# Where the row maxima of attention logits are read from: PSUM banks in halves, or the SBUF copies in one piece

## The chip, the cores and the metric

The kernel runs on one core of a Trainium2 chip. The metric is device time in microseconds (us). The kernel before has a median of 3184.22 us over three runs (3184.0 to 3186.14). The core's engines run side by side, each through its own queue in order: TensorE (PE, matmuls; its weight loads are shown as PEld), VectorE (DVE), ScalarE (ACT), GpSimd (POOL), and SyncE (SP), which issues the transfers.

## The reference

Input: 8 images of 512 channels and 32x32 pixels, float32. Two pre-activation layers follow each other, each `x + f(groupnorm(x))`:

- Layer 0: a 1x1 convolution with SiLU to 2 x 256 channels, then two bottleneck blocks on 256 channels, and a 1x1 convolution over the four collected results. Each block is a 3x3 convolution with SiLU, an attention over the 1024 pixels with 4 heads of 64 channels, a 1x1 convolution with SiLU, and a residual sum.
- Layer 1: a grouped 1x1 convolution with scaled, masked and permuted weights, brought to one dense 512x512 matrix.

The attention is what matters here. For each head:

```
logits = einsum('bhdi,bhdj->bhij', q, k + r) * HD ** (-0.5)     # 1024 queries x 1024 keys
a = softmax(logits, axis=-1)
out = einsum('bhij,bhdj->bhdi', a, v)
```

The softmax subtracts, for each query, the largest logit over all 1024 keys.

## The kernel before

Everything is float32. An attention is cut into units: `Unit(im, i, hp, half)` handles a pair of heads (hp) and half of the queries (512) of one block of one image. There are 8 x 2 x 2 x 2 = 64 units. The logits of a unit lie transposed, keys on partitions and queries along the columns, in eight key tiles of 128 keys. One key tile is two heads of 512 queries: 1024 columns.

In `logits` (lines 500 to 523) each key tile `t` takes two PSUM banks, one for each head, from the pool `ps_f` of five banks that all matmuls of the kernel share in turn. PE writes both (L511). ACT copies each bank to its half of an SBUF tile `st` (L518; ten `st` buffers in the pool `stp`). From the second key tile on, DVE takes an elementwise maximum into `mx` (L523), one instruction for each head.

After the last key tile, `top` (L531, L532) has PE transpose `mx`, and DVE reduces each transposed piece to the negative maximum over the 128 partitions, `nm`. `spread` (L540) broadcasts that into two PSUM banks of their own, `mb`. For each key tile `soften` (L545) adds `mb` to `st` on DVE, `exponent` (L549) takes the exponential in place on ACT, and POOL adds the result to a running sum `acc` (called `sum` in the profile) in four pieces of 256 columns (L556). `values` (L563) multiplies by v into the accumulator `po`. `finish` (L577, L580) and `divide` (L584, L586) form the denominator and divide.

The main loop works on key tiles in pairs and on two units at once. A step for `t, t+1` issues, in this order: `soften(t)` and `soften(t+1)` of the present unit u, `exponent(t)`, `values` of the pair before, `logits(t)` and `logits(t+1)` of the next unit, and `exponent(t+1)`. So DVE's maxima belong to the next unit while POOL's sums belong to the present one. The ten `st` buffers mean that tiles t and t+1 of the next unit go into the slots of tiles t-2 and t-1 of the present one, which must have been read by `values` and by POOL's sums.

Between the steps, matmuls of other stages are woven in by `advance`, out of a list that `slot_filler` makes for each slot of four units: the convolutions `cv`, `l`, `m2`, the 3x3 convolution of the coming block in a transformed form (`conv3`, L313, products `m`), and its projection. The input transform of `conv3` (`transform`, L280 to L288) is eight DVE instructions of 544 columns that read SBUF only, spread in time by due times of a planner's clock. The order on DVE is partly written down: `in_turn` chains the maxima, the softening and the transform. `act_turn` and `pe_turn` do the same for ACT's copies and exponentials and for PE's attention matmuls. The rest is placed by order of issue.

Dependencies are turned into semaphores automatically. [...] where ACT and DVE both read a bank, the second reader waits for the first, and the bank can be written again when both are done.

Of the kernel before, what the change touches and what calls it, by code (L numbers as in the profile page):

```python
# [17 lines left out]
ALU = mybir.AluOpType  # L18
# [21 lines left out]
def conv_preact_kernel(ctx: ExitStack, tc: tile.TileContext, x, cv1, cv2, mcv1, qkv, mcv2, bn, rw, rh, conv, s_in, t_in, out):  # L40
    nc = tc.nc
# [23 lines left out]
    def pair(p, tag, name):  # L65
        return p.tile([P, 2, HALF], F32, tag=tag, name=name)

    def bank(name):
        return ps_f.tile([P, HALF], F32, tag="bank", name=name)
# [4 lines left out]
    def flat(t):  # L74
        return t.rearrange("p a b -> p (a b)")
# [106 lines left out]
    def in_turn(instruction):  # L182

        if turn:
            tc.add_manual_dep(instruction.ins, turn.pop().ins.name, IN_ORDER, reason="order of VectorE")
        turn.append(instruction)

    def act_turn(instruction):

        if act_last:  # L190
            tc.add_manual_dep(instruction.ins, act_last.pop().ins.name, IN_ORDER, reason="order of ScalarE")
        act_last.append(instruction)
# [3 lines left out]
    def pe_turn(instruction):  # L196

        if pe_last:
            tc.add_manual_dep(instruction.ins, pe_last.pop().ins.name, IN_ORDER, reason="order of TensorE")
        pe_last.append(instruction)  # L200
# [293 lines left out]
    class Unit:  # L494
# [8 lines left out]
        def logits(self, t):  # L503

            if t == 0:
                self.begin()
            lg = [bank(f"lg_{self.name}_{t}_{h}") for h in range(2)]
            for h in range(2):
                r = slice(HD * h, HD * h + HD)
                pe_turn(  # L510
                    nc.tensor.matmul(  # L511
                        lg[h], self.k[r, ts(t, P)], self.q[r, self.hp, ts(self.half, HALF)], start=True, stop=True
                    )
                )
            st = pair(stp, "st", f"st_{self.name}_{t}")
            self.st.append(st)
            for h in range(2):
                act_turn(nc.scalar.copy(st[:, h], lg[h]))  # L518
            if t == 1:
                self.mx = pair(one, "mx", f"mx_{self.name}")  # L520
            for h in range(2 if t else 0):
                so_far = self.st[0] if t == 1 else self.mx
                in_turn(nc.vector.tensor_tensor(self.mx[:, h], so_far[:, h], lg[h], ALU.max))  # L523

        def top(self):

# [621 lines left out]
```

## Time and profile before

| | |
|---|---|
| median of three runs | 3184.22 us |
| the profiled execution | 3188.51 us |
| its span, first to last instruction | 3186.8 us |
| mean granted clock of TensorE | 0.993 |
| PE busy | 3085.9 us (97%) |
| DVE busy | 2050.6 us (64%) |
| ACT busy | 1717.3 us (54%) |
| POOL busy | 1395.3 us (44%) |
| DVE maxima, L523 | 896 instructions of 512 columns |
| POOL sums, L556 | 1792 instructions of 256 columns |

A group line of the profile names the source line, the engine and operation, what is written from what, the shapes and the count; after the first bar stand the busy time in us and the mean of one in ns; after the second bar stands the engine's idle time before these instructions and what ended it. A line of a timeline starts with the start time in us and the duration; several instructions of one kind are merged (x4), and square brackets show idle time of the engine before them, with what ended it. The wait view gives, for an engine and a line, what it waited for: us in total, times, and the longest.

### The profile page before, as it was taken

What the parts mean: (1) busy time and instruction counts of PE and PEld (TensorE: products, weight loads), DVE (VectorE), ACT (ScalarE), POOL (GpSimd) and SP (SyncE); (2) the same over time, 40 slices, a digit from 0 to 9 for tenths busy, and PEclk for the clock granted to TensorE, in tenths of its full rate; (3) what the DMA queues carried; (4) which work ended last, traced back from release to release, by engine and by line L of the source; (5) the groups of instructions that cost most, each with busy time, mean ns of one, the idle gap of its engine ahead of it and who ended that gap; (6) DMA issues with size and microseconds to landing.
All of it is one profiled execution on the core that took longest, in us unless ns stands there. A gap on an engine that the chain in (4) does not pass through costs nothing.

```text
span 3186.8 us, 34171 instructions
## 1 busy us (share of the span) xinstructions
PE 3085.9 (97%) x11668; PEld 1522.9 (48%) x11668; DVE 2050.6 (64%) x2718; ACT 1717.3 (54%) x2347; POOL 1395.3 (44%) x1867
## 2 busy tenths in 40 slices
PE   7999999999999999999999999999999999999999
PEld 3645444454445454454445454454445454453333
DVE  5446576667666676667666676667766676666742
ACT  3255765854655555544656455554656455555631
POOL 2114444446444454445444454355434454455420
PEclk9999999999999999999999999999999999999999
DMA  8851442421233232424233332424233332413366
GB/s 294 287 187 63 154 161 83 149 79 65 88 109 129 93 119 70 148 86 137 89 109 129 119 114 75 139 83 142 90 113 132 110 122 71 145 63 129 110 212 216
DMA packets 142014, 399.35 MB, mean 125 GB/s; under 512 B 13072, under 2 KB 14352, under 8 KB 141840
## 3 DMA queue, kind: packets, MB, share of 16 engines
q1 hardware_dynamic: 141120, 396.94, 36.4%
q8 instruction: 92, 1.51, 0.2%
q14 instruction: 82, 0.67, 0.1%
q10 hardware_dynamic: 720, 0.23, 0.0%
HBM read 317.42 MB, written 79.69 MB: 125 GB/s over the span
## 4 chain that ended last, share of the span: by engine, by line
PE 70%; DVE 7%; ACT 5%; issue 3%; DMA 2%; POOL 1%; ACTq 0%; DVEq 0%; SPq 0%; POOLq 0%
PE m L313 14%; PE cv L175 12%; PE lg L511 11%; PE po L563 11%; PE qk L175 6%; PE l L175 6%; PE v L405 3%; PE m L175 2%; DVE st L545 2%; PE mb L540 2%; ACT st L518 2%; PE mt L531 2%; PE den L577 2%; DVE mx L523 1%; ACT st L549 1%
## 5 line engine op out<-in xcount | busy, mean ns | idle before, releaser
L556 POOL TENSOR_TENSOR sum<-sum,st 128x256 f32<-128x256 f32 x1536 | 1126.1, 767 | 570.1 <-ACT st L549 565.0
L523 DVE TENSOR_TENSOR mx<-mx,lg 128x512 f32<-128x512 f32 x768 | 477.8, 681 | 412.2 <-ACT st L518 412.2
L549 ACT ACTIVATE st<-st 128x1024 f32<-128x1024 f32 x512 | 539.1, 1068 | 340.2 <-DVE st L545 338.8
L518 ACT COPY st<-lg 128x512 f32<-128x512 f32 x1024 | 524.4, 596 | 351.7 <-PE lg L511 306.6
L545 DVE TENSOR_TENSOR st<-st,mb 128x1024 f32<-128x1024 f32 x512 | 603.7, 1213 | 63.6 <-PE mb L540 63.6
L313 PE MATMUL m<-plane,w_m 128*128 128x256 f32 x2304 | 537.4, 388 | 21.8 <-DVE x2r L487 9.0
L556 POOL TENSOR_TENSOR sum<-st,st 128x256 f32<-128x256 f32 x256 | 188.0, 766 | 789.4 <-ACT st L549 789.3
L563 PE MATMUL po<-st,v 128*64 128x512 f32 x2048 | 500.3, 608 | 21.7 <-ACT st L549 14.7
L511 PE MATMUL lg<-q,k 64*128 64x512 f32 x2048 | 513.7, 619 | 1.6 <-ACT y L130 1.5
L313 PEld LDWEIGHTS m<-plane,w_m 128*128 128x128 f32 x2304 | 433.0, 192 | 149.0 <-issue 44.1
L175 PE MATMUL cv<-y,w_cv 128*128 128x512 f32 x1024 | 465.4, 599 | 10.8 <-DVE mx L523 6.2
L511 PEld LDWEIGHTS lg<-q,k 64*128 64x128 f32 x2048 | 178.6, 187 | 330.1 <-issue 266.4
L175 PEld LDWEIGHTS cv<-y,w_cv 128*128 128x128 f32 x1024 | 185.7, 190 | 251.7 <-issue 227.8
L563 PEld LDWEIGHTS po<-st,v 128*64 128x64 f32 x2048 | 128.9, 137 | 327.5 <-issue 228.9
L175 PE MATMUL l<-x,w_l 128*128 128x512 f32 x512 | 235.8, 603 | 10.3 <-DVE mx L523 10.0
L175 PE MATMUL cv<-x,w_cv 128*128 128x512 f32 x512 | 233.4, 603 | 8.5 <-ACT x L165 2.4
L175 PE MATMUL qk<-z,w_qkv 128*128 128x512 f32 x512 | 234.0, 600 | 1.7 <-DVE mx L523 1.7
L584 DVE RECIPROCAL rb<-rb 128x256 f32<-128x256 f32 x128 | 215.4, 1723 | 30.6 <-ACT rb L580 30.5
L532 DVE TENSOR_REDUCE nm<-mt 128x4 f32<-128x512 f32 x128 | 82.4, 685 | 158.6 <-PE mt L531 158.5
L580 ACT COPY rb<-den 128x512 f32<-128x512 f32 x64 | 37.3, 583 | 226.9 <-PE den L577 226.9
L175 PEld LDWEIGHTS l<-x,w_l 128*128 128x128 f32 x512 | 92.7, 190 | 132.3 <-issue 107.2
L175 PEld LDWEIGHTS cv<-x,w_cv 128*128 128x128 f32 x512 | 94.3, 192 | 126.4 <-issue 107.3
(145 smaller groups left out, 2404.3 us busy)
## 6 DMA issues: line engine op xcount, KB each, us to landing
w_m<-w_m SPq DMA_DIRECT2D x96, 768.0 KB, 4.8
w_cv<-in_cv SPq DMA_DIRECT2D x90, 512.0 KB, 3.5
y<-y SPq DMA_DIRECT2D x64, 512.0 KB, 4.4
x<-in_x SPq DMA_DIRECT2D x56, 512.0 KB, 5.4
y<-y SPq DMA_DIRECT2D x64, 256.0 KB, 3.5
k<-r SPq DMA_DIRECT2D x32, 512.0 KB, 3.6
res<-y SPq DMA_DIRECT2D x32, 512.0 KB, 4.0
xr<-in_x SPq DMA_DIRECT2D x32, 512.0 KB, 4.0
```

The source lines that it names most:

```text
L175: nc.tensor.matmul(ps, w, moving, start=(n == 0), stop=(n == len(terms) - 1))
L313: nc.tensor.matmul(ps[:, ts(co, 256)].rearrange("p (t x) -> p t x", x=F), w[:, co, c, dx], u[:, 9 * c : 9 * c + 8, dx : dx + F], start=(j ...
L405: nc.tensor.matmul(ps[:, ts(j, P)], z[:, c, ts(4 * j4 + j, P)], w[:, c, 512 + P * hp : 512 + P * hp + P], start=(c == 0), stop=(c == IT - 1),)
L511: nc.tensor.matmul(lg[h], self.k[r, ts(t, P)], self.q[r, self.hp, ts(self.half, HALF)], start=True, stop=True)
L518: act_turn(nc.scalar.copy(st[:, h], lg[h]))
L523: in_turn(nc.vector.tensor_tensor(self.mx[:, h], so_far[:, h], lg[h], ALU.max))
L532: nc.vector.tensor_reduce(self.nm[:, h], mt, AX.X, ALU.max, negate=True)
L545: in_turn(nc.vector.tensor_tensor(st, st, flat(self.mb), ALU.add))
L549: act_turn(nc.scalar.activation(st, st, AF.Exp))
L556: nc.gpsimd.tensor_tensor(flat(self.acc)[:, part], flat(so_far)[:, part], st[:, part], ALU.add)
L563: nc.tensor.matmul(self.po[HD * h : HD * h + HD], self.v[:, t, ts(h, HD)], self.st[t][:, h], start=(t == 0), stop=(t == KT - 1),)
L584: nc.vector.reciprocal(self.rb[:, r], self.rb[:, r])
```

## The change

The maxima read the SBUF copies `st` instead of the PSUM banks `lg`, and one instruction covers both heads: 1024 columns for each key tile. `flat` views a tile of 2 x 512 as 1024 columns. The first maximum of a unit (t = 1) takes `st[0]` and `st[1]`. Nothing else is edited.

```diff
             if t == 1:
                 self.mx = pair(one, "mx", f"mx_{self.name}")
-            for h in range(2 if t else 0):
+            if t:
+
                 so_far = self.st[0] if t == 1 else self.mx
-                in_turn(nc.vector.tensor_tensor(self.mx[:, h], so_far[:, h], lg[h], ALU.max))
+                in_turn(nc.vector.tensor_tensor(flat(self.mx), flat(so_far), flat(st), ALU.max))
```

## The prediction

> **What bounds the kernel now.** I read the page's shares first, then the costliest groups, then what PE waited for, then the stretches around those waits.
>
> ```profile
> PE 3085.9 (97%) x11668; PEld 1522.9 (48%) x11668; DVE 2050.6 (64%) x2718; ACT 1717.3 (54%) x2347; POOL 1395.3 (44%) x1867
> ...
> L556 POOL TENSOR_TENSOR sum<-sum,st 128x256 f32<-128x256 f32 x1536 | 1126.1, 767 | 570.1 <-ACT st L549 565.0
> L523 DVE TENSOR_TENSOR mx<-mx,lg 128x512 f32<-128x512 f32 x768 | 477.8, 681 | 412.2 <-ACT st L518 412.2
> ...
> L545 DVE TENSOR_TENSOR st<-st,mb 128x1024 f32<-128x1024 f32 x512 | 603.7, 1213 | 63.6 <-PE mb L540 63.6
> ```
>
> PE is busy for all but 100.9 us of the span. About 26 us of that lie in the head and tail; some 75 us lie between 180 and 3060 us, in stalls of up to 3.7 us. Only there can this change move the time. The maxima already wait for ACT's copy (all 412.2 us of their idle time), because both read one bank. So waiting for the copy is not new.
>
> ```profile
> PE l L175 <- DVE mx L523: 10.0, 5, 2.6
> ...
> PE cv L175 <- DVE mx L523: 8.2, 7, 2.0
> ...
> PE po L563 <- DVE mx L523: 6.9, 8, 2.3
> ...
> PE m L313 <- DVE mx L523: 2.1, 5, 1.5
> ...
> PE qk L175 <- DVE mx L523: 1.7, 1, 1.7
> ```
>
> PE waits for a bank that a maximum still reads: l, cv, m and qk, 18 waits, 22.0 us. The eight of po need no bank of that pool; in the timeline each starts within 0.1 us of the end of an exponential, so I count them to ACT.
>
> What makes the maxima late is seen in a stretch with a 1.47 us stall:
>
> ```profile
> 1612.60 1.25 DVE L283 TENSOR_TENSOR plane<-a,b 128x544 f32<-128x544 f32 x1
> ...
> 1613.77 1.24 DVE L285 TENSOR_TENSOR a<-ybuf 128x544 f32<-128x544 f32 x1
> 1614.94 2.34 DVE L545 TENSOR_TENSOR st<-st,mb 128x1024 f32<-128x1024 f32 x2
> ...
> 1617.38 7.34 POOL L556 TENSOR_TENSOR sum<-sum,st 128x256 f32<-128x256 f32 x8 [2.95 <-ACT st L549]
> ...
> 1619.57 2.46 DVE L523 TENSOR_TENSOR mx<-mx,lg 128x512 f32<-128x512 f32 x4
> ...
> 1624.06 2.34 DVE L545 TENSOR_TENSOR st<-st,mb 128x1024 f32<-128x1024 f32 x2
> ...
> 1626.27 2.02 ACT L518 COPY st<-lg 128x512 f32<-128x512 f32 x4
> ...
> 1627.61 2.84 PE L175 MATMUL cv<-y,w_cv 128*128 128x512 f32 x6 [1.47 <-DVE mx L523]
> ```
>
> DVE has no gap from 1611 to 1626: transform, softening, maxima, softening. The second softening releases the exponential, the copies stand behind that on ACT, and the bank comes free last. The transforms make such stretches, four in each run of about 720 us (a pair of images); the later runs repeat nearly the same stalls. Elsewhere (1526 to 1545 us) PE is busy 19.00 of 19 us and DVE 11.69.
>
> [...]
>
> ```profile
> L286 DVE TENSOR_TENSOR b<-ybuf x16: 712/1242/1248, 62.3 to 2762.0; 128x544 f32<-128x544 f32 x16
> ```
>
> With both inputs in SBUF it takes 712 ns, or about 1242 (minimum, median, maximum), and nothing later: +0.53 us. The maxima with one input in PSUM stay within 634 to 690 ns although POOL is active for half of their time. [...]
>
> **The change part by part.** Sums are against the profiled execution, 3188.5 us, and carried to the median, which is 4.3 us lower.
>
> *Fewer, longer instructions.* Back to back, halves start 598 ns apart and 1024-column softenings 1131 ns apart (medians of the trace). So 448 x (2 x 598 - 1131) ns = 29 us less DVE work, if nothing disturbs. On PE's path that is 0.13 us for each pair of key tiles, in the transform stretches alone.
>
> *Two SBUF inputs.* No row shows this instruction at 1024 columns. Lower bound: the softening, 1.13 to 1.22 us. Upper: 0.53 us more, 1.75[...]. POOL is active in 50% of the maxima's time before, more after; I take 1.5 us on average. DVE then gains 448 x 0.5 x 0.53 = 119 less 29, about 90 us of work (64% to 67%). POOL in turn waits. A 544-column DVE instruction (0.72 us) lengthens a sum from 727 to 1180-1286 ns, so 0.2 us less than its own length; 1024 columns should cost some 0.95 us: 224 x 0.95 = 210 us, 44% to 50%.
>
> *A later start.* A maximum now needs both halves copied: 0.5 us later than its first half had. Where DVE is idle, the last one of a unit ends some 1.5 us after the last copy instead of 1.04; with contention 2.6. PE's transposes follow 3.2 us after the last maximum by median; in nine units it is less than 1.3. Of these, two have POOL active: 0.78 at 751.8 us, which costs about 0.8 us, and 1.27 at 255.1, about 0.3. The other seven (1.12 to 1.26) are uncontended, and matmuls of other stages hide the 0.45. If that cover were gone, 0.5 to 1.6 us in each of 64 units.
>
> *Banks freed at the copy's end.* A maximum ends 0.72 us (least) to 1.08 us (mean) after the copy of its bank. Of the 18 waits I credit 0.7 us each or all of it: five l 3.5, seven cv 4.7, five m 1.35, one qk 0.7: 10 us. What is late next is the copy itself, behind the exponential.
>
> *What the contention does in the transform stretches*, read from the run of 1130 to 1630 us:
> - 1132 to 1145: the pair of maxima starts 0.5 later and costs 0.9 more under eight POOL sums; POOL drags on, so one residual sum and L283, undisturbed before, each lose 0.5. The stall at 1142 is released by ACT behind the exponential, not by a maximum: +2.4, no credit.
> - 1308 to 1333: copy-released stalls gain 0.6 and 0.2, but the maxima at 1321 start late and run into the next sums, and L283 and L288 after them; the stall at 1331, behind x2r (L487) on DVE, grows 1.7: net +0.9.
> - 1447 to 1458: maxima +0.9, L285 +0.3, less the bank's 0.7: +0.5.
> - 1619 to 1628: +0.9 and +0.2 less 0.7: +0.4.
>
> That is 4.2 us, and four such runs, 17 us. The bank credits of these stretches are inside. To it come the early part's free credits at 341, 439 and 526 us, -2, and the tight place at 720 to 760 us, +3 (transposes above; denominators that follow the last sum by 0.65 and 0.71 us, so a later POOL shows). Sum +18. A stall that grows gives DVE and POOL time to catch up before the next, as at 1320 and 1331, so I take off a quarter: +13. Forecast 3201.5 profiled, 3197 median, range of this case 3191 to 3210.
>
> Behind each maximum on DVE stand the softening, x2r and the transform; for softening waits ACT's exponential, for that `values` on PE. In plain steps 7 us of spare DVE time in each 19 cover the extra 1 us of each pair; without it each pair would cost 1 us.
>
> **The rivals.**
>
> 1. *The bank credit wins* (faster). Place: the bank waits; price: up to 10 us, plus stalls after them. For it: 18 named waits, five banks, and a mean hold of 1.08 us after the copy. Against: in the same stretches DVE is full and POOL active. It decides if a contended maximum costs under about 0.3 us more instead of 0.53, or if POOL is mostly idle there. Time 3184 - 10 = 3174.
> 2. *It cancels* (within 0.2%, 6.4 us, about what a measurement of this kernel can tell from no change). Half the +17 absorbed, credits kept: +0 to +5, about 3186. For: PE busy 97%, so most DVE time is off the path.
> 3. *POOL becomes late for the slots* (much slower). Copies already wait 45.0 us in 23 cases for sums. A copy of tile 5 starts 2.3 us after the sum of tile 3 has freed its slot, by median, 1.4 in one case of ten. Two maxima push POOL by 1.9. If half the 64 units lost 1 us on PE, +32, with +13 above: 3229. Against: banks come free 1 us earlier, which lets copies be that late, and tiles 4 and 6 have at least 3.2 us of slack.
>
> That the change doesn't do what it says I exclude: same maxima, same order chain, and no new wait for the copies.
>
> **How the numbers follow.** Forecast case 0.50, late POOL 0.10: slower 0.60. Cancelling 0.23, credit 0.17. The range reaches down to the credit's price nearly (3176) and up halfway to the POOL case (3216); about 0.1 is left on each side.
>
> **What would show it.** The L523 row: 448 instructions, minimum near 1.2 us, many near 1.75, mean 1.4 to 1.6; at 1.22 throughout, step two is wrong. POOL's mean over 800 ns, DVE busy 2100 to 2180. PE's waits on mx gone or on ACT's copy instead; stalls like 1142 and 1331 longer. The forecast fails if stalls of that kind stay as they are, or if copies waiting for sums grow well past 45 us.

## The result and the profile after

The changed kernel takes 3225.86 us by median (3222.3 to 3230.61), against 3184.11 us: a ratio of 1.0128, 95% interval 1.0112 to 1.0143. It is slower by 42 us, where 13 were forecast, and lies above the range. The profiled execution took 3222.3 us, with a span of 3220.6 us, 33.8 us more than before. Below line 521 the line numbers are one higher than before (L524 is the maximum, L557 the sums).

The page of the changed kernel, shares and groups:

```profile
PE 3099.1 (96%) x11668; PEld 1526.8 (47%) x11668; DVE 2143.2 (67%) x2270; ACT 1715.7 (53%) x2347; POOL 1665.0 (52%) x1867
...
L557 POOL TENSOR_TENSOR sum<-sum,st 128x256 f32<-128x256 f32 x1536 | 1388.6, 939 | 416.2 <-ACT st L550 416.1
L524 DVE TENSOR_TENSOR mx<-mx,st 128x1024 f32<-128x1024 f32 x384 | 551.8, 1437 | 431.3 <-ACT st L518 409.5
...
L546 DVE TENSOR_TENSOR st<-st,mb 128x1024 f32<-128x1024 f32 x512 | 603.6, 1213 | 64.9 <-PE mb L541 63.3
```

Half as many maxima take more time than before, and the sums, which nobody edited, take 939 ns in the mean instead of 767. POOL's busy time grew by 270 us and DVE's by 93 us. The lines of those two instructions (minimum, median and maximum in ns behind the count) show that it is a matter of two groups, not of a general slowing:

```profile
L524 DVE TENSOR_TENSOR mx<-mx,st x384: 1176/1562/1837, 189.3 to 3053.5; 128x1024 f32<-128x1024 f32 x192
...
L557 POOL TENSOR_TENSOR sum<-sum,st x1536: 712/727/1799, 233.2 to 3090.0; 128x256 f32<-128x256 f32 x192
```

The median of the sums is still 727 ns; those that meet a maximum take up to 1.8 us.

What PE waited for in the changed kernel:

```profile
PE po L564 <- ACT st L550: 22.8, 19, 3.7
PE m L313 <- ACT cv2s L130: 13.7, 3, 4.6
...
PE l L175 <- ACT st L518: 13.4, 5, 3.6
PE m L313 <- ACT st L518: 10.2, 11, 2.3
...
PE m L313 <- DVE z L367: 5.3, 7, 1.2
```

The waits for a bank that a maximum reads are gone. In their place stand waits for ACT's copy (l, m) and for DVE's output of conv3 (z): the copy itself has become late. I compared the start of the same matmul in the two traces. The distance grows in steps, at the same places in each run of a pair of images. In the stretch that was 1687 to 2225 us before, the steps above 0.35 us are as follows (the second column names PE's product, then what it waits for; cv2s, x2r and z are outputs whose making frees a bank):

| before, us | PE waits, in the changed kernel, for | step, us |
|---|---|---|
| 1687 | m: ACT's copy of logits (new) | +0.77 |
| 1719 | m: DVE's z, L367 (new) | +1.13 |
| 1863 | m: ACT's cv2s | +1.77 |
| 1985, 2028 | cv: nothing any more | -0.82, -0.72 |
| 2041 | l: ACT's copy | +0.86, then +1.68 at a PEclk of 0.50 |
| 2053 | m: x2r | -0.37 |
| 2099 | m: DVE's z (new) | +0.51 |
| 2174 to 2179 | lg, l | +0.57 |
| 2225 | m: ACT's copy (new) | +1.63 |

They add up to 7.0 us. Over the whole execution the distance is 5.7 us at 546 us and grows by 5.8 from 700 to 785 us, by 7.7 from 785 to 1504, by 7.9 from 1504 to 2225 and by 6.4 from there to the end.

### The profile page after: what moved, and what is told of

It reads as the page before. It is cut to its first block, busy times and chain, and to the rows that moved or that the text cites. A ratio compares the mean times of both kernels' runs of the same rounds, so it can differ in the third digit from the quotient of the medians.

```text
span 3220.6 us, 33438 instructions
## 1 busy us (share of the span) xinstructions
PE 3099.1 (96%) x11668; PEld 1526.8 (47%) x11668; DVE 2143.2 (67%) x2270; ACT 1715.7 (53%) x2347; POOL 1665.0 (52%) x1867
## 4 chain that ended last, share of the span: by engine, by line
PE 72%; DVE 9%; ACT 6%; issue 3%; DMA 2%; POOL 2%; SPq 0%; ACTq 0%; DVEq 0%; POOLq 0%
PE cv L175 14%; PE m L313 11%; PE po L564 11%; PE lg L511 11%; PE qk L175 7%; PE l L175 6%; PE v L405 3%; ACT st L518 3%; DVE mx L524 3%; PE m L175 2%; PE den L578 2%; DVE st L546 2%; PE mb L541 2%; PE mt L532 2%; POOL sum L557 2%
## 5 line engine op out<-in xcount | busy, mean ns | idle before, releaser
L557 POOL TENSOR_TENSOR sum<-sum,st 128x256 f32<-128x256 f32 x1536 | 1388.6, 939 | 416.2 <-ACT st L550 416.1
L524 DVE TENSOR_TENSOR mx<-mx,st 128x1024 f32<-128x1024 f32 x384 | 551.8, 1437 | 431.3 <-ACT st L518 409.5
L557 POOL TENSOR_TENSOR sum<-st,st 128x256 f32<-128x256 f32 x256 | 194.6, 792 | 717.2 <-ACT st L550 717.2
```

The source lines that it names most:

```text
L524: in_turn(nc.vector.tensor_tensor(flat(self.mx), flat(so_far), flat(st), ALU.max))
L557: nc.gpsimd.tensor_tensor(flat(self.acc)[:, part], flat(so_far)[:, part], st[:, part], ALU.add)
```

## The experiments

### Is it the second SBUF input or the grain?

Theory: DVE and POOL take turns (contention). Rival: one long instruction that starts later (grain). Four runs, in two pairs: the maxima from SBUF in halves, and the three forms without POOL's sums over the key tiles.

```diff
-                in_turn(nc.vector.tensor_tensor(self.mx[:, h], so_far[:, h], lg[h], ALU.max))
+                in_turn(nc.vector.tensor_tensor(self.mx[:, h], so_far[:, h], st[:, h], ALU.max))
```

> The maxima read the SBUF copies, but stay in halves of 512 columns, each behind its own copy. Contention theory (the second SBUF input makes DVE take turns with POOL's sums): each half can wait 0.53 us, so a pair of key tiles that meets the sums costs up to 4.5 us instead of 3.3; at least as slow as the change, 3225 to 3260 us; the halves fall into two groups, near 0.68 and near 1.2 us. Grain theory (the loss comes from one long instruction that waits for both copies and ends later): with the halves back the loss goes, 3174 to 3190 us.

Measured: 3255.79 us, ratio 1.0208 (1.0186 to 1.0229). Its maxima (view by line):

```profile
L523 DVE TENSOR_TENSOR mx<-mx,st x768: 666/1207/1867, 187.7 to 3089.5; 128x512 f32<-128x512 f32 x192
```

The median is 1207 ns, 0.53 us more than the 681 ns from PSUM: about half now take that much longer beside a sum, and there are two of them for each key tile. So the wide instruction is the better of the two forms, as long as POOL runs.

For the next three the sums are reduced to eight short additions on the second tile, so that the denominators are not the softmax's:

```diff
-            for j in range(4 if t else 0):
-
-                part = slice(256 * j, 256 * j + 256)
-                so_far = self.st[0] if t == 1 else self.acc
-                nc.gpsimd.tensor_tensor(flat(self.acc)[:, part], flat(so_far)[:, part], st[:, part], ALU.add)
+            for j in range(8 if t == 1 else 0):
+
+                part = slice(128 * j, 128 * j + 128)
+                nc.gpsimd.tensor_tensor(flat(self.acc)[:, part], st[:, part], ones, ALU.add)
```

> The kernel before, with POOL's sums over the key tiles left out: only a short one on the second tile remains, so the denominators are not the softmax's. It is the base for the two runs beside it. Both theories: the transform no longer takes turns with POOL, so the stalls of its stretches shrink: 3150 to 3175 us.

> The changed kernel with POOL's sums left out in the same way. Contention theory: every maximum takes about 1.22 us, and the change is worth what its two good parts are worth: 0 to 10 us faster than the kernel before without sums. Grain theory: the loss stays, 10 to 40 us slower than the kernel before without sums.

> Halves from SBUF and no sums: against the kernel before without sums only the bank is freed earlier, by the copy alone. Contention theory: 3 to 10 us faster than the kernel before without sums, which is the price of the bank. Grain theory: the same 3 to 10 us; it tells the bank's part from the grain's, as the difference to the 1024-column run.

Measured: 3152.51 us (3151.37 to 3155.22) for PSUM halves, 3151.24 (3150.63 to 3152.49) for the change, 3148.21 (3147.66 to 3150.11) for SBUF halves. In the changed form:

```profile
L524 DVE TENSOR_TENSOR mx<-mx,st x384: 1170/1225/2342, 187.9 to 2983.5; 128x1024 f32<-128x1024 f32 x192
```

The whole loss is gone with the sums: the change as such costs nothing. The bank freed by the copy is worth 4.3 us (3152.51 to 3148.21), less than half of the 10 I had credited, and the wide instruction gives 3.0 of them back. The grain theory falls as the cause of the 42 us.

### Whose time is it: DVE's turns, or the late sums?

The same taking of turns makes DVE wait and POOL late. Pieces of another size were to shift the weight between the two:

```diff
-            for j in range(4 if t else 0):
+            for j in range(8 if t else 0):
-                part = slice(256 * j, 256 * j + 256)
+                part = slice(128 * j, 128 * j + 128)
```

> The changed kernel with POOL's sums in eight pieces of 128 columns instead of four of 256. Turn theory (what costs is that DVE waits out one POOL instruction's reading): a disturbed maximum waits half as long, 1.45 to 1.5 us instead of 1.75, and the loss shrinks by a third or more: 3195 to 3215 us. Late-POOL theory (what costs is that the sums end later, so that slots and denominators are late): POOL gets more instructions and is later still, 3230 to 3260 us.

Measured: 3276.5 us, ratio 1.0287 (1.0249 to 1.0325). Most of the disturbed maxima did fall, to between 1.4 and 1.6 us, yet 20 took 2.2 to 7.3 us, and the time rose by 51 us. The waits of this run, its maxima, and one stretch:

```profile
ACT st L518 <- POOL sum L557: 114.2, 61, 4.2
...
DVE plane L346 <- POOL plane L344: 52.3, 11, 5.8
...
L524 DVE TENSOR_TENSOR mx<-mx,st x384: 1206/1294/7332, 186.3 to 3100.4; 128x1024 f32<-128x1024 f32 x192
...
3123.90 14.44 POOL L557 TENSOR_TENSOR sum<-sum,st 128x128 f32<-128x128 f32 x35
...
3126.90 11.12 DVE L150 TENSOR_TENSOR gd_b<-mv_b,gms_b 128x4 f32<-128x4 f32 x1
```

The turn theory's time is wrong, for two reasons. POOL is later: L346 waits 52.3 us for conv3's subtraction (37.9 in the changed kernel), and copies wait 114.2 us for sums (24.0). And DVE doesn't always wait for one sum alone: an instruction of only 4 columns (L150, 0.16 us elsewhere) stood for 11.12 us until the row of sums was nearly through. Beside the changed kernel's trace, six stalls of m at conv3's places make 28.8 of the growth, with the slower clock behind them (a mean granted clock of 0.984 against 0.990), and three places where a DVE instruction stood for 6.6 to 11.1 us make 21.3.

> The changed kernel with the sums in two pieces of 512 columns. Turn theory: a disturbed maximum waits 1.07 us, 2.2 to 2.3 us in all: 3230 to 3275 us. Late-POOL theory: POOL has less fixed cost and ends earlier: 3195 to 3220 us.

Measured, with two pieces of 512: 3253.09 us, ratio 1.0203 (1.0184 to 1.0222). The disturbed maxima take up to 2.29 us, DVE's busy time is 2221.6 us, and copies wait only 12.3 us for sums. It is 27 us slower than the change although POOL is less busy (1470.2 us) and L346 waits only 17.1 us, so here DVE's longer waits cost the time, and not POOL's lateness. Pieces of 256 are the best of the three sizes.

Two kernels share out the key tiles, by the part of their maxima's time that met a sum before:

```diff
+            if t in (1, 5, 7):
+                in_turn(nc.vector.tensor_tensor(flat(self.mx), flat(so_far), flat(st), ALU.max))
+            else:
+                for h in range(2 if t else 0):
+                    in_turn(nc.vector.tensor_tensor(self.mx[:, h], so_far[:, h], lg[h], ALU.max))
```

> Key tiles 1, 5 and 7 take the maximum from SBUF in one instruction; 2, 3, 4 and 6 from PSUM in halves, as before. In the profile before, POOL was active in 7, 36 and 33% of these tiles' maxima, and in 91, 70, 55 and 53% of the others', so they hold 0.76 of 3.45 parts of the overlap. Contention theory: about that share of the 42 us, +9: 3186 to 3200 us. A theory that the loss comes from a unit's last maximum (tile 7), which the transposes wait for: 3210 to 3225 us.

> The counterpart: key tiles 2, 3, 4 and 6 from SBUF in one instruction, 1, 5 and 7 from PSUM in halves. Contention theory: 2.69 of 3.45 parts of the 42 us, +33: 3205 to 3225 us. Last-maximum theory: 3180 to 3195 us.

Measured: 3201.18 us, ratio 1.0035 (1.0022 to 1.0048), and, for tiles 2, 3, 4 and 6, 3199.19 us, ratio 1.0037 (1.0024 to 1.0049). The first is near what contention gives, the second is not: a share of 78% of the overlap brought 29% of the loss. The two together cost 0.72%, the whole change 1.28%. The loss is not proportional to the overlap. In the trace of the second, the new stalls on ACT's copy at 784, 1504 and 2225 us add 0.7 us each, where the whole change added 1.6 to 1.8, and those at 968, 1687 and 2408 are not there. That fits a stall that begins only once the delay is longer than the spare time of its place. With tile 1 alone:

> Only key tile 1 takes its maximum from SBUF in one instruction; in the profile before POOL was active in 7% of that tile's maxima. Contention theory: no loss and nearly no gain, since few bank waits fall on it: 3181 to 3188 us. Grain theory: one seventh of 42 us, 3188 to 3192 us.

Measured: ratio 0.9997 (0.9988 to 1.0005), no difference.

### The queue behind POOL

The trace of the changed kernel shows one path by which late sums reach PE. Its timeline in the stretch whose bank wait at 1522.93 us is new:

```profile
1507.42 10.71 POOL L557 TENSOR_TENSOR sum<-sum,st 128x256 f32<-128x256 f32 x12
...
1518.09 1.32 POOL L344 TENSOR_TENSOR plane<-ybuf 128x544 f32<-128x544 f32 x1
...
1519.45 0.73 DVE L346 SCALAR_TENSOR_TENSOR plane<-b,plane 128x544 f32<-128x544 f32 x1 [4.13 <-POOL plane L344]
1520.09 2.35 DVE L546 TENSOR_TENSOR st<-st,mb 128x1024 f32<-128x1024 f32 x2
...
1522.31 2.03 ACT L518 COPY st<-lg 128x512 f32<-128x512 f32 x4
...
1522.93 3.29 PE L313 MATMUL m<-plane,w_m 128*128 128x256 f32 x14 [1.48 <-ACT st L518]
```

The same step in the kernel before:

```profile
1497.37 1.33 POOL L344 TENSOR_TENSOR plane<-ybuf 128x544 f32<-128x544 f32 x1
1498.73 0.73 DVE L346 SCALAR_TENSOR_TENSOR plane<-b,plane 128x544 f32<-128x544 f32 x1 [2.76 <-POOL plane L344]
...
1499.38 2.34 DVE L545 TENSOR_TENSOR st<-st,mb 128x1024 f32<-128x1024 f32 x2
...
1500.89 5.45 PE L313 MATMUL m<-plane,w_m 128*128 128x256 f32 x24
```

L344 is a subtraction that conv3 leaves to POOL. It stands behind twelve sums, three of them stretched (1.72, 1.71 and 1.20 us). L346 needs it and, since it stands ahead of the softening on DVE, holds that up although DVE is idle for 4.13 us; behind the softening come the exponential, the copies and the bank. The test moves L343 and L344 to DVE, in both kernels:

```diff
-            nc.gpsimd.tensor_tensor(inner(u0), d[0], d[2], ALU.subtract)
-            nc.gpsimd.tensor_tensor(inner(u5), d[5], d[3], ALU.subtract)
+            nc.vector.tensor_tensor(inner(u0), d[0], d[2], ALU.subtract)
+            nc.vector.tensor_tensor(inner(u5), d[5], d[3], ALU.subtract)
```

> The changed kernel with the two subtractions of conv3 that POOL makes (L343, L344: 16 times each) moved to DVE. In the changed kernel's trace L344 stands behind POOL's stretched sums, L346 on DVE waits for it, and the softening, the exponential, the copies and a bank behind that. Queue theory (part of the loss goes through these two instructions): the stalls of products m on ACT's copies, 10.2 us, go: 8 to 15 us faster than the change, 3211 to 3218 us. Plain-load theory (only DVE's own turns count): DVE gets 32 x 0.7 to 1.2 us more work in the fullest stretches: 3226 to 3240 us.

> The same move in the kernel before, as the base. There the sums are shorter and L344 delays L346 less (31.4 us in 11 waits, against 37.9). Queue theory: 3180 to 3190 us, so that the distance between the two is 27 to 34 us instead of 42. Plain-load theory: 3184 to 3195 us, the distance stays near 42.

Measured: 3210.59 us, ratio 1.0072 (1.0056 to 1.0089), and for the kernel before 3187.36 us, ratio 1.0002 (0.9994 to 1.0011). The changed kernel gains 15 us although DVE has more to do (2173.4 us busy); the kernel before gains nothing. The waits of PE in the changed kernel with the move:

```profile
PE m L313 <- DVE z L367: 5.8, 7, 1.2
...
PE m L313 <- ACT st L518: 3.1, 1, 3.1
```

Of the eleven waits for ACT's copy one is left. With the move in both kernels, the steps of +0.77 and +1.63 are no longer there in the comparison of matmul starts; those at 1719 (+1.15) and 1863 us (+1.85) are, and the one at 2041 is larger (+1.98). So about 44% of the loss (1.28% less 0.72; the intervals leave a quarter to three fifths) went through two instructions that the change does not touch.

### What is left: each half by itself

An idle load on DVE, with one SBUF input, POOL untouched: evenly, behind each key tile's maxima, and in lumps of 384 columns behind tiles 2, 3 and 4.

```diff
+            if t:
+                in_turn(nc.vector.tensor_reduce(spare, ident, AX.X, ALU.max))
```

> The kernel before with one idle reduction of 128 columns (one SBUF input, the identity) behind each key tile's maxima: 448 x about 0.2 us, near the 92.6 us by which DVE's busy time grew with the change; POOL is left alone, the banks are freed as before. DVE theory (the 23 us of loss left without the queue through POOL's planes are DVE's added time in the full stretches): 3200 to 3212 us. POOL theory (they come from the sums' lateness in other places): 3184 to 3193 us.

> The kernel before with the same idle load on DVE as in the evenly loaded run (some 90 us, one SBUF input), but in lumps of about 0.47 us behind the maxima of key tiles 2, 3 and 4 alone, where the change's maxima meet the sums most. Lump theory (the rest of the loss is DVE's added time, and it is dearer where it falls together): 3200 to 3212 us. POOL theory (the rest needs the sums to be late): near the evenly loaded run, 3190 to 3199 us.

Measured: DVE busy 2139.0 us and ratio 1.0033 (1.0024 to 1.0042); 2134.4 us and ratio 1.0006 (0.9994 to 1.0018). DVE's added time alone, of the change's size, costs 0.33 and 0.06% in these two forms. Both fell short of the DVE theory's 3200 us and more; the lumps were not dearer than the even load, against the lump theory.

Then POOL made late, the maxima untouched (the kernel before with sums of 128 columns), the same with conv3's subtractions on DVE, and sums of 512:

> The kernel before with POOL's sums in eight pieces of 128 columns. Its transform and residual sums take turns with POOL too; leaving the sums out was worth some 33 us. Turn theory: these wait 0.27 us instead of 0.53, a gain of 3 to 10 us: 3174 to 3182 us. Late-POOL theory: the sums take 1613 us instead of 1374 and are late for the slots: 3190 to 3215 us.

> The kernel before with POOL made late by other means (sums in pieces of 128, which cost it 20 us without touching the maxima), and conv3's two subtractions moved from POOL to DVE. Queue theory (late sums reach PE mostly through these two instructions): most of the 20 us go, 3186 to 3195 us. If late sums reach PE by other ways (slots, denominators): 3200 to 3212 us.

> The kernel before with the sums in two pieces of 512 columns: DVE's transform and residual sums wait 1.07 us where they meet one, instead of 0.53, and POOL spends some 160 us less. DVE theory: the waits are doubled in the full stretches, 3188 to 3205 us. POOL theory: earlier sums win, 3172 to 3183 us, which would beat the kernel before.

Measured: ratio 1.0063 (1.0048 to 1.0078) with POOL busy 1672.7 us, nearly the changed kernel's 1665.0; with the move 1.0029 (1.0018 to 1.0040); with sums of 512, 1.0009 (1.0003 to 1.0016). These runs do not give the price of late sums alone. DVE's busy time grew too (2087.9 us with pieces of 128), for here again DVE stood behind whole rows of sums: gd_b (L150, 4 columns) for 12.27 us, go_a (L162, 4 columns) for 6.58. The stalls of PE at these two places, with what follows them, make +7.9 us at 565 and +11.8 at 3051 in the comparison of matmul starts, more than the 15.7 us by which the profiled span grew; from 785 to 2930 us the distance fell by 8. Both instructions stand as long with the move (6.59 and 12.74 us). Of the 10.1 us of span that the move saved there, 9 lie at the six places of conv3 where L345 had stood for about 6 us. The hope that finer sums would beat the kernel before by shorter turns fell too.

What stays open is how the other 23 us divide. DVE's added time alone costs 0.06 to 0.33% where it was tried; the price of late sums alone, without longer waits of DVE, was not measured. The traces name the places (1719, 1863, 2041). No kernel here beat the kernel before while computing all of it.

## Why the prediction was right or wrong

**Right: the sign and the source of the loss.** Two SBUF inputs (halves of 1207 ns by median, against 681 with one in PSUM), turns with POOL's sums (up to 1.80 us instead of 0.73), and DVE late where PE waits. With the sums gone, the loss is gone (3151.24 us against 3152.51). The ways by which it reaches PE are in part others than forecast.

**Right: the sizes of the parts.** Maxima: forecast 1.2 us undisturbed, up to 1.75, mean 1.5; measured 1.18 and up to 1.84, mean 1.44 (the first maximum of a unit 1.27, four of the 64 at 2.02 to 2.22). DVE: forecast +90 us, measured +93; that they agree so well is in part luck, since the maxima account for 73 and other DVE instructions that met more sums for the rest. POOL: forecast +210, measured +270, over a quarter more.

**Right in the transform stretches, in sum.** Forecast 4.2 us for the run read: +2.4 at 1142, +0.9 at 1308 to 1333, +0.5 at 1447 to 1458, +0.4 at 1619 to 1628. Measured: +1.8 (the stall went from 2.71 to 4.56 us), +1.8, +0.5 and -0.1, together 3.9. The sum is nearer than its terms, which is luck. The tight place, 720 to 760 us, was put at +3; from 700 to 783 us the distance grew by 3.9.

**Wrong: the step "In plain steps 7 us of spare DVE time in each 19 cover the extra 1 us of each pair".** This is where the prediction failed: it put the steps outside these stretches at nothing. From 785 to 1504 us four places there took 4.05 us (968: +0.77, 999: +1.13, 1378: +0.51, 1504: +1.64), more than half of the 7.7 by which the distance grew; from 1504 to 2225 four took 4.04 of 7.9. An average of spare time covers nothing at a place where DVE has none. The runs show two such kinds of place.

The first is a chain on DVE itself. Its spare time lies ahead of the maxima, where they wait for ACT's copy; from there to z (L367) it has no gap. The step at 1719, before and after:

```profile
1711.39 2.48 DVE L523 TENSOR_TENSOR mx<-mx,lg 128x512 f32<-128x512 f32 x4 [2.89 <-ACT st L518]
...
1718.08 0.68 DVE L367 TENSOR_TENSOR z<-m,ss 128x512 f32<-128x512 f32 x1
```

```profile
1732.06 3.31 DVE L524 TENSOR_TENSOR mx<-mx,st 128x1024 f32<-128x1024 f32 x2 [3.97 <-ACT st L518]
...
1739.38 0.68 DVE L367 TENSOR_TENSOR z<-m,ss 128x512 f32<-128x512 f32 x1
...
1740.12 3.08 PE L313 MATMUL m<-plane,w_m 128*128 128x256 f32 x13 [1.17 <-DVE z L367]
```

The distance was 20.2 us there, so the pair of maxima starts 0.5 us later and takes 0.8 longer, and the bank that z frees comes 1.1 us later for PE.

The second is the queue behind POOL. I counted POOL's lateness for slots and denominators, and not for the two instructions of conv3 that POOL executes between the sums, though the change pushes the sums and the trace of before already showed L346 waiting for L344. Of the 7.0 us in the table, 2.4 are steps of this kind (1687, 2225) and 1.6 of the first (1719, 2099). The move of L343 and L344 took away the second kind, left the first, and gave back 15 us in the whole kernel.

**Wrong: the early part.** The forecast had -2 us of credits ahead of 546 us; measured +5.7. The credited stalls at 341 and 526 did go (-2.2, -1.9), but the one at 439 grew (1.49 to 2.30 us), and others added more, at 218 us (+4.2), 255 (+1.5) and 347 (+3.9).

**Wrong: the stretch 1308 to 1333.** I had the copy-released stall gain 0.2; it grew by 1.22, 0.86 and 2.06 in three runs. The second maximum is now one piece and stands behind a residual sum that waits for a transfer, where three of four halves had passed before. The growth I put at x2r (+1.7) was +1.28 once and then -0.4.

**Missing: TensorE's clock.** A long PE stall can be paid twice. The windows of the changed kernel behind such a stall (us, busy time of PE, PEld, DVE, ACT and POOL, then PEclk, DMA share and GB/s):

```profile
2060.00:2066.00 6.00, 2.54 (x7) 0.73 (x6) 3.90 (x5) 5.98 (x11) 3.64 (x4) 0.92 0.95 339
2066.00:2070.00 4.00, 4.00 (x15) 1.22 (x16) 4.00 (x4) 3.30 (x3) 3.92 (x4) 0.70 0.03 12
```

The eight matmuls of po there took 3.14 us instead of 1.94. The stall here was 3.46 us; at the same place in the kernel before it was 2.60, and PEclk 1.00 behind it. Yet in the kernel before, PEclk is 0.50 from 1323 to 1326 us, behind a stall of only 2.24. So the length of one stall does not settle it, and what does is not shown. The mean clock fell from 0.993 to 0.990: 1% of 3220.6 less 0.7% of 3186.8 is 10 us, an upper bound, since part of it passes in stalls.

**Wrong: a quarter taken off** because a stall lets others catch up. Some do, as x2r at 2053 (-0.37), but the whole is more than its parts: the two mixes cost 0.72% together, the change 1.28.

**The bank credit** was 4.3 us instead of 10, measured where nothing else disturbs.

**The rivals.** The late-POOL rival named a time (3229 us) near the result, but not its path: copies waited 24.0 us for sums after the change, less than the 45.0 before, so the slots did not carry it. With finer sums copies waited 114.2 us; how much of that run's loss went this way was not measured. The credit and cancelling cases are excluded by the interval.

## What to carry to other kernels

Before a DVE instruction gets a second SBUF input, look at what POOL does at the same time (here the halves went from 681 to 1207 ns by median), and then at what else stands in POOL's queue: here part of the lateness came out where DVE waits for that (at L346 37.9 us, where it was 31.4), not only where the two meet. Slack that a busy share shows (DVE was busy for 64% before) counts only at the place where it lies: not behind the last wait of a chain, and not where the next instruction in the queue waits for another engine. And where a stall grows to 2 us and more, look at the clock behind it: here the matmuls that followed ran at half clock behind some stalls of 2.1 to 4.6 us, and not behind all.

## What was not expected of the hardware

A sum of 256 columns that meets a 1024-column maximum takes up to 1.80 us instead of 0.73: it grows by 1.07, nearly the whole length of a maximum (1.18 at the least). The maximum, 1.23 us where POOL is idle, takes up to 1.84 beside sums, so it grows by 0.61 at most, less than one sum's 0.73, even where twelve sums stand in a row (1.43 and 1.57 there); the four of 2.02 to 2.22 stood beside one of conv3's subtractions as well. With sums of 128 columns that no longer holds: a DVE instruction of 4 columns stood for up to 12.27 us, until a row of sums was nearly through, and maxima for up to 7.33. Why it then gets no turn between two sums is not shown. The kernel before loses 1.15% (ratio 0.9885, 0.9864 to 0.9906, without the sums) to POOL's sums beside DVE and to what waits for them, with the maxima read from PSUM. Neither finer nor longer pieces gained any of it.
